# Local attention on one core: weighted values by features, weights divided before their transposition, one wide exponential, and another order of TensorE's stages

## The chip, the cores and the metric

The kernel runs on one core of a Trainium2 chip. The metric is the time of one execution on the device, in microseconds; less is better. TensorE multiplies and transposes, ScalarE (ACT) and VectorE (DVE) empty its results out of PSUM and do the elementwise work, GpSimd (POOL) takes elementwise work between tiles in SBUF, and SyncE (SP) issues the DMAs.

## What is computed

All data are float32. The input is 8 sequences of 512 tokens with 128 features. First comes a linear attention with a Taylor feature map (16 heads), then six layers of local attention and feed-forward. The change lies in the local attention:

```python
H, HD, W = 16, 64, 32                      # heads, features of a head, window
for i in range(6):
    x = attn_layer(shift_tokens(x), Wqkv[i], q_scale[i], k_scale[i], Wo[i]) + x
    x = ffn_layer(shift_tokens(x), ...) + x

# attn_layer: project, unit length and scale of q and k, rotary, then in windows of 32 tokens
sim  = einsum('bhwie,bhwje->bhwij', bq, bk2) * 8     # 32 queries by 64 keys (own and last window)
sim  = where(mask, -max, sim)
attn = softmax(sim, -1)
out  = einsum('bhwij,bhwje->bhwie', attn, bv2)
return out.reshape(b, n, 1024) @ Wo
```

## The kernel before

After the linear attention the kernel works in blocks of 128 tokens. There are 4 blocks in a sequence, 8 sequences and 6 layers: 192 blocks. The running activations stay in SBUF, features by tokens, one `state` tile for each sequence.

The steps of a block are functions, and one loop over t calls them, each with a lag: `at(t, lag, step)` runs a step for block t - lag. So one pass of the loop holds steps of several blocks, and it is what the document calls a block's time. TensorE's instructions are issued in exactly the order in which this loop writes them (`manual_schedule` for PE). The other engines' orders are made by a scheduler; `tc.high_priority()` and `issue_behind(later, earlier)` push it. Every engine runs its own list strictly in order.

The steps, with their lags before the change:

- `proj` (lag 0, twice: for q and for k): two matmuls into a PSUM tile of tag "mm" (line 451). VectorE makes the two rotary products from it (lines 459 and 467), ScalarE two squares (line 475), POOL adds the products (line 482).
- `sum_squares`, `unit_length` (lag 0): VectorE sums the squares (line 485); ScalarE takes Ln and Exp (lines 96 and 98); POOL clips (line 495) and multiplies q and k by it (line 498).
- `values`, `spread` (lag 0): two matmuls into "mm" (line 509), one copy by ScalarE (line 514), then 10 DMAs (8 and two memsets in a sequence's first block) that lay the windows out in `v2` with heads of even pairs on partitions 0 to 63 and of odd ones on 64 to 127.
- `by_features` (lag 1): 16 transposes of q and k, in four PSUM tiles of tag "tr" with four transposes each (line 70), each emptied by a ScalarE copy (line 548). POOL copies the last 32 tokens' keys for the next block (line 551).
- `masked`, `scores` (lag 1): ScalarE writes the mask into a PSUM tile of tag "s" (line 558), 64 small matmuls add the scores `sp` to it (line 572); VectorE takes the negated maxima (line 580); ScalarE takes 16 exponentials with the maxima as bias (line 584, 64 columns each); VectorE sums and inverts (lines 590 and 591).
- `by_keys`, `weigh_values` (lag 2): 8 transposes of the weights `pe`, in two "tr" tiles, copied by ScalarE (line 602); 64 small matmuls weigh the values into `po`, tokens by features, tag "s" (line 613); VectorE divides by the sums (line 621) into `on`.
- `out_by_features` (lag 2): 8 transposes of `on` in two "tr" tiles, copied by ScalarE (line 635).
- `out_project` (lag 3): 8 matmuls into `py`, tag "s" (line 642); VectorE adds it to the state (line 647).
- Feed-forward, in a sequence's last block alone, so each in one pass of four: `feed_norm` (4 transposes `nx` of the state into "mm", statistics by VectorE, lines 107 and 109, Ln and Exp by ScalarE, lines 96 and 98, normalising by VectorE, line 112), `feed_first` (4 transposes), `feed_middle` (six matmuls, lines 667 and 669, with Gelu at 673, for which ScalarE loads another table, and loads the old one back, lines 76 and 82), `feed_last` (three matmuls, line 702).

PSUM has three tags: "mm" with two buffers of 4 KB a partition, "tr" with two of 2 KB, "s" with one of 4 KB. A stage that takes a buffer waits until the tile before the last one of its tag has been read. A float32 matmul shows as two matmul records, each with its load of weights.

`addr_align` puts filler instructions into TensorE's list (lines 668, 671, 780 and 782).

Of the kernel before, what the change touches and what calls it, by code (L numbers as in the profile page):

```python
# [15 lines left out]
P = 128  # L16
# [7 lines left out]
FILL = 16  # L24
IN_STEP = 98
# [3 lines left out]
def sandwich_kernel(ctx: ExitStack, tc: tile.TileContext, ins: dict, out: bass.AP):  # L29
# [43 lines left out]
    tables, exps, divisions, copies, pcopies, maxima = [], [], [], [], [], []  # L73
# [365 lines left out]
    def proj(u, s):  # L439

        L, b, j = u["L"], u["b"], u["j"]
        wqkv, tab = L["wqkv"], L["tab"]
        lhs = state[b][:, j * P : (j + 1) * P]
        if s == 0:
            u["ss"] = f2.tile([P, 2, H], F32, tag="ss", name="ss")
            u["qk"] = f2.tile([P, 2, H, 2, HF], F32, tag="qk", name="qk")
        ss, qk = u["ss"], u["qk"]

        ps = psum.tile([P, 2, H, HF], F32, tag="mm", name="mm")
        for a in range(2):  # L450
            nc.tensor.matmul(  # L451
                ps[:, a].rearrange("p h d -> p (h d)"), lhs, wqkv[:, s, a, :], start=True, stop=True
            )
        sq = f2.tile([P, H, 2, HF], F32, tag="sq", name="sq")
        t1 = f2.tile([P, 2, H, HF], F32, tag="t1", name="t1")
        t2 = f2.tile([P, 2, H, HF], F32, tag="t2", name="t2")

        def turned():
            nc.vector.tensor_tensor(  # L459
                t2, ps[:, ::-1],  # L460
                tab[:, 2 * s + 1, j, :].rearrange("p (a d) -> p a d", a=2).unsqueeze(2)
                .to_broadcast([P, 2, H, HF]),
                ALU.mult,
            )

        def straight():
            nc.vector.tensor_tensor(  # L467
                t1, ps,
                tab[:, 2 * s, j, :].rearrange("p (a d) -> p a d", a=2).unsqueeze(2)
                .to_broadcast([P, 2, H, HF]),  # L470
                ALU.mult,
            )

        def squared(a):
            nc.scalar.activation(sq[:, :, a, :], ps[:, a], AF.Square)  # L475

        turned()
        straight()
        squared(0)
        squared(1)  # L480
        u["sq", s] = sq
        nc.gpsimd.tensor_tensor(qk[:, s].rearrange("p h a d -> p a h d"), t1, t2, ALU.add)  # L482

    def sum_squares(u, s):
        su = nc.vector.tensor_reduce(  # L485
            u["ss"][:, s], u["sq", s].rearrange("p h a d -> p h (a d)"), AX.X, ALU.add
        )
        if divisions:
            issue_behind(su, divisions[-1])
# [22 lines left out]
    def spread(u):  # L512
        j, v0 = u["j"], u["v0"]
        cp = nc.scalar.copy(v0, u.pop("v0ps"))
        if copies:
            issue_behind(cp, copies[-1])
# [36 lines left out]
    def masked(u):  # L553
# [7 lines left out]
        issue_behind(sd, copies[-1])  # L561

    def scores(u):
# [18 lines left out]
        for pair in range(NP):  # L582
            for p in range(2):
                ex = nc.scalar.activation(  # L584
                    pe[:, pair, p, :], sp[:, p, pair, :], AF.Exp, bias=mx[:, p, pair : pair + 1]
                )
                issue_behind(ex, tables[-1])
        exps.append(ex)
        su = f2.tile([P, NP, 2], F32, tag="su", name="su")
        nc.vector.tensor_reduce(su, pe, AX.X, ALU.add)  # L590
        nc.vector.reciprocal(su, su)
        u["pe"], u["su"] = pe, su
# [11 lines left out]
    def weigh_values(u):  # L604


        v2, pT, su = u["v2"], u["pT"], u["su"]
        po = psum.tile([P, 2, NP, HD], F32, tag="s", name="po", bufs=1)
        for pair in range(NP):
            for w in range(4):  # L610
                for p in range(2):
                    r = slice(HD * p, HD * (p + 1))
                    nc.tensor.matmul(  # L613
                        po[W * w : W * (w + 1), p, pair, :],
                        pT[r, pair, W * w : W * (w + 1)],
                        v2[r, w, HD * pair : HD * (pair + 1)],
                        start=(pair == 0), stop=True, skip_group_check=True,
                    )
        u["on"] = on = f1.tile([P, NP, 2, HD], F32, tag="on", name="on")
        with tc.high_priority():  # L620
            dv = nc.vector.tensor_tensor(
                on.rearrange("t c p d -> t p c d"), po,
                su.rearrange("t c p -> t p c").unsqueeze(3).to_broadcast([P, 2, NP, HD]), ALU.mult,
            )
        divisions.append(dv)

    def out_by_features(u):
        on = u["on"]
        u["oT"] = oT = f1.tile([P, NP, P], F32, tag="oT", name="oT")
        for c in range(0, NP, 4):  # L630
            ps = psum.tile([P, 4, P], F32, tag="tr", name="tr")
            for i in range(4):
                transposed(ps[:, i, :], on[:, c + i].rearrange("p a d -> p (a d)"), P, P)
            with tc.high_priority():
                nc.scalar.copy(oT[:, c : c + 4, :], ps)  # L635

    def out_project(u):

        L, b, j, oT = u["L"], u["b"], u["j"], u["oT"]
        py = psum.tile([P, P], F32, tag="s", name="py", bufs=1)  # L640
        for c in range(NP):
            nc.tensor.matmul(py, L["wo"][:, c, :], oT[:, c, :], start=(c == 0), stop=(c == NP - 1))  # L642
# [7 lines left out]
    def feed_norm(u):  # L650
# [6 lines left out]
        u["normed"] = layer_norm(f2, xn, ps, NB, by_log=True, later=True)  # L657
# [4 lines left out]
    def feed_hidden(u, c):  # L662
# [5 lines left out]
        nc.tensor.addr_align(FILL, offset=FILL // 2)  # L668
        nc.tensor.matmul(pg[:cn, 1], w1[:, c0 : c0 + cn], xnT, start=True, stop=True)  # L669
        if c < NCH - 1:  # L670
            nc.tensor.addr_align(FILL, offset=FILL // 2)
# [85 lines left out]
    with tc.manual_schedule(engines={mybir.EngineType.PE}):  # L757
# [8 lines left out]
        for t in range(len(units) + 7):  # L766
# [6 lines left out]

            gelus = 0 <= t - 5 < len(units) and units[t - 5]["j"] == NB - 1
            at(t, 0, proj, 0)
            at(t, 0, proj, 1)


            if t % NB == 1 and NB < t < len(units):
                nc.tensor.addr_align(128, offset=IN_STEP)  # L780
            if t % NB == 3 and NB < t < len(units):
                nc.tensor.addr_align(FILL)
            at(t, 2, by_keys)
            if gelus:
                gelu_only()
            at(t, 3, out_project)
# [6 lines left out]
            at(t, 2, weigh_values)  # L793
            at(t, 1, by_features, 4, 0)
            at(t, 1, masked)
            at(t, 0, values)
# [6 lines left out]
            at(t, 1, by_features, 4, 1)  # L803
            at(t, 0, spread)
            at(t, 3, feed_norm, ends=True)
            at(t, 4, feed_first, ends=True)

            ends = 9 + NB * B * (DEPTH - 1) <= t < len(units) + 5
            after = 10 + NB * B * (DEPTH - 1) <= t < len(units) + 6
            if after:  # L810
                at(t, 10, out_roots, ends=True)
            if ends:
                at(t, 9, out_by_tokens, ends=True)
                at(t, 9, out_stats, ends=True)
            at(t, 5, feed_middle, ends=True)
            if gelus:
                at(t, 0, unit_length)
            at(t, 6, feed_last, ends=True)
            at(t, 1, scores)
            if after:  # L820
                at(t, 10, store, ends=True)
            if t == len(units) + 5:
                at(t, 6, out_by_tokens)
                at(t, 6, out_stats)
                at(t, 6, out_roots)
                at(t, 6, store, False)
            at(t, 3, feed_normed, ends=True)
            at(t, 2, out_by_features)


# [98 lines left out]
```

## Time and profile before

| what | value |
|---|---|
| runs | 3638.80, 3639.42, 3642.14 us; median 3639.42 |
| span of the profiled execution | 3641.2 us |
| mean granted TensorE clock | 0.993 of full speed |
| first projection of the local attention | 479.0 us after the start |
| busy in 600 to 3500 us, of 2900: PE, DVE, ACT, POOL | 2892, 2351, 2356, 1708 us |
| sixteen transposes of q and k, `tr<-ident,qk` | 3072 of 276 ns mean |
| division, line 621 | 192 of 1225 ns |
| exponentials, line 584 | 3072 of 381 ns, 652.0 us busy |

The profiled execution's own time is not given beside its span; its span lies inside the three runs, 0.9 us under the longest. A group's row gives busy time (overlaps counted once), the mean length of one instruction, then the idle time ahead of it and what ended that. Matmuls are pipelined, so the mean length of one is far above the distance from one to the next. A timeline's row gives start, length, engine, line, tile and how many instructions are merged in it.

### The profile page before, as it was taken

To read this page: it belongs to the slowest core of one execution; us is meant where nothing else is said; L and a number is where in the kernel's file an instruction comes from. 1 tells how busy PE (TensorE), PEld (TensorE's weight loads), DVE (VectorE), ACT (ScalarE), POOL (GpSimd) and SP (SyncE) were. 2 spreads that over 40 slices of the span, in tenths; PEclk is the share of its full clock that TensorE was granted. 3 is DMA by queue.
4 is the path that set the end of the run, shared out by engine and by line. 5 is a ranking of instruction groups with operands and counts; after the bars stand their busy time and mean duration, and the time that the engine had idled before them with its cause. 6 is when DMAs were issued, how large, how long until landed. Compare 5 with 4: busy or idle time off the path is not lost.

```text
span 3641.2 us, 153034 instructions
## 1 busy us (share of the span) xinstructions
PE 3575.2 (98%) x65184; PEld 2404.3 (66%) x65184; DVE 2796.4 (77%) x3915; ACT 2765.6 (76%) x6864; POOL 1843.6 (51%) x1311
## 2 busy tenths in 40 slices
PE   8999989999999999999999999999999999999997
PEld 4555556666766666676766766667676676766765
DVE  4555567887878788787887878878787887878885
ACT  4555557787888888888787888888878787887875
POOL 0000045555655556555565655556555565556652
PEclk9999999999999999999999999999999999999998
DMA  3121132222232222232222322223222222222221
GB/s 109 46 53 47 42 89 68 65 65 69 79 77 72 65 64 71 77 81 68 61 69 68 87 72 69 65 65 86 71 71 69 60 70 64 66 68 73 74 74 47
DMA packets 158598, 250.73 MB, mean 69 GB/s; under 512 B 33774, under 2 KB 54508, under 8 KB 157164
## 3 DMA queue, kind: packets, MB, share of 16 engines
q1 hardware_dynamic: 157932, 240.93, 25.2%
q8 instruction: 530, 8.68, 1.0%
q14 instruction: 136, 1.11, 0.1%
HBM read 41.31 MB, written 4.46 MB: 13 GB/s over the span
## 4 chain that ended last, share of the span: by engine, by line
PE 87%; ACT 9%; DVE 2%; issue 1%; DMA 1%; POOL 0%; SPq 0%; POOLq 0%; DVEq 0%; ACTq 0%
PE tr L70 19%; PE mm L451 14%; PE py L642 10%; PE mm L509 9%; PE po L613 8%; PE sp L572 6%; ACT pe L584 4%; PE mm L667 4%; PE mm L669 4%; PE y L299 3%; PE py L702 3%; PE sc L269 2%; PE po L348 2%; ACT L76 1%; PE vv L247 1%; ACT oT L635 1%
## 5 line engine op out<-in xcount | busy, mean ns | idle before, releaser
L482 POOL TENSOR_TENSOR qk<-t,t 128x1024 f32<-128x1024 f32 x384 | 910.9, 2372 | 619.1 <-DVE t L467 424.7
L498 POOL TENSOR_TENSOR qk<-qk,ss 128x1024 f32<-128x1024 f32 x384 | 722.4, 1902 | 16.0
L451 PE MATMUL mm<-wqkv,state 128*128 128x512 f32 x1536 | 700.3, 596 | 0.6 <-issue 0.6
L584 ACT ACTIVATE pe<-sp,mx 128x64 f32<-128x64 f32 x3072 | 652.0, 381 | 2.4 <-DVE mx L580 2.3
L459 DVE TENSOR_TENSOR t<-mm,tab 128x1024 f32<-128x1024 f32 x384 | 468.3, 1219 | 220.3 <-PE mm L451 214.9
L475 ACT ACTIVATE sq<-mm 128x512 f32<-128x512 f32 x768 | 420.6, 605 | 127.4 <-DVE t L467 120.9
L467 DVE TENSOR_TENSOR t<-mm,tab 128x1024 f32<-128x1024 f32 x384 | 468.1, 1219 | 5.9
L451 PEld LDWEIGHTS mm<-wqkv,state 128*128 128x128 f32 x1536 | 273.1, 190 | 289.8 <-issue 242.4
L485 DVE TENSOR_REDUCE ss<-sq 128x16 f32<-128x1024 f32 x384 | 448.4, 1209 | 0.1
L70 PE MATMUL tr<-ident,qk 128*128 128x128 f32 x3072 | 440.9, 276 | 1.8 <-ACT qT L548 0.8
L70 PEld LDWEIGHTS tr<-ident,qk 128*128 128x128 f32 x3072 | 351.3, 141 | 120.7 <-issue 56.3
L642 PE MATMUL py<-oT,wo 128*128 128x128 f32 x3072 | 379.3, 277 | 0.3 <-ACT oT L635 0.3
L642 PEld LDWEIGHTS py<-oT,wo 128*128 128x128 f32 x3072 | 368.1, 196 | 0.5 <-ACT oT L635 0.5
L509 PE MATMUL mm<-wqkv,state 128*128 128x512 f32 x768 | 362.9, 595 | 2.6 <-DVE t L467 2.6
L635 ACT COPY oT<-tr 128x512 f32<-128x512 f32 x384 | 205.5, 587 | 168.1 <-PE tr L70 165.5
L572 PEld LDWEIGHTS sp<-kT,qT 64*32 64x32 f32 x24576 | 264.2, 105 | 91.3 <-issue 54.3
L613 PE MATMUL po<-v,pT 64*32 64x64 f32 x24576 | 297.0, 225 | 9.6 <-issue 3.9
L548 ACT COPY qT<-tr 128x512 f32<-128x512 f32 x384 | 226.3, 589 | 99.6 <-PE tr L70 99.1
L613 PEld LDWEIGHTS po<-v,pT 64*32 64x32 f32 x24576 | 268.8, 105 | 46.0 <-PE tr L70 24.6
L572 PE MATMUL sp<-kT,qT 64*32 64x64 f32 x24576 | 297.6, 225 | 0.3 <-issue 0.3
L495 POOL TENSOR_SCALAR ss<-ss 128x32 f32<-128x32 f32 x192 | 54.7, 285 | 478.7 <-ACT ss L98 470.8
L548 ACT COPY kT<-tr 128x512 f32<-128x512 f32 x384 | 225.6, 588 | 74.8 <-PE tr L70 74.5
(110 smaller groups left out, 5243.9 us busy)
## 6 DMA issues: line engine op xcount, KB each, us to landing
v<-v SPq DMA_DIRECT2D x1152, 128.0 KB
v<-v SPq DMA_DIRECT2D x672, 64.0 KB
rs<-roots SPq DMA_DIRECT2D x64, 256.0 KB
wqkv<-in_L_ffn_Wqkv_dram SPq DMA_DIRECT2D x6, 1536.0 KB
wo<-in_L_ffn_Wo_dram SPq DMA_DIRECT2D x6, 512.0 KB
xin<-_attn_hidden_states_dram SPq DMA_DIRECT2D x8, 256.0 KB
xr<-_attn_hidden_states_dram SPq DMA_DIRECT2D x8, 256.0 KB
x<-xr SPq DMA_DIRECT2D x8, 256.0 KB
```

Source lines behind the costliest of these rows:

```text
L70: nc.tensor.transpose(ps[:cols, :rows], src, ident[:rows, :rows])
L451: nc.tensor.matmul(ps[:, a].rearrange("p h d -> p (h d)"), lhs, wqkv[:, s, a, :], start=True, stop=True)
L459: nc.vector.tensor_tensor(t2, ps[:, ::-1], tab[:, 2 * s + 1, j, :].rearrange("p (a d) -> p a d", a=2).unsqueeze(2) .to_broadcast([P, 2, H, ...
L467: nc.vector.tensor_tensor(t1, ps, tab[:, 2 * s, j, :].rearrange("p (a d) -> p a d", a=2).unsqueeze(2) .to_broadcast([P, 2, H, HF]), ALU.mult,)
L482: nc.gpsimd.tensor_tensor(qk[:, s].rearrange("p h a d -> p a h d"), t1, t2, ALU.add)
L498: nc.gpsimd.tensor_tensor(t, t, ss[:, i, :].unsqueeze(2).to_broadcast([P, H, HD]), ALU.mult)
L509: nc.tensor.matmul(ps[:, p, :], lhs, L["wqkv"][:, 2, p, :], start=True, stop=True)
L548: copies.append(nc.scalar.copy(dst, ps))
L572: nc.tensor.matmul(sp[W * w : W * (w + 1), p, pair, :], qT[HD * p : HD * (p + 1), pair, W * w : W * (w + 1)], kT[HD * p : HD * (p + 1), pa ...
L584: ex = nc.scalar.activation(pe[:, pair, p, :], sp[:, p, pair, :], AF.Exp, bias=mx[:, p, pair : pair + 1])
L613: nc.tensor.matmul(po[W * w : W * (w + 1), p, pair, :], pT[r, pair, W * w : W * (w + 1)], v2[r, w, HD * pair : HD * (pair + 1)], start=(pa ...
L642: nc.tensor.matmul(py, L["wo"][:, c, :], oT[:, c, :], start=(c == 0), stop=(c == NP - 1))
```

## The change

- The weights are divided by their sums (in a new step `divided`, lag 2, on POOL) before `by_keys` transposes them. The maxima are subtracted by VectorE, and one exponential of 128x1024 runs in place.
- `weigh_values` takes the values as stationary operand and the weights as moving one, so that `po` comes out as features by tokens, in a tile of tag "mm". One ScalarE copy of 128x1024 makes `oT` from it; `out_by_features` with its transposes is gone. The rows of `Wo` are put in another order on the host to fit.
- `py` moves from tag "s" to "tr". `nx` is copied to SBUF by ScalarE and normalised from there.
- The filler instructions are gone, as is an ordering of the sums of squares behind the division and one of the value copy behind the copies of q and k; the mask is ordered behind the squares.
- The order of the stages in a pass and their lags are new: the sixteen transposes of q and k stand together, `by_keys` lies between the two projections (lag 3), `values` comes at the end with lag 2, and what follows has one lag more.

```diff
     def scores(u):
...
-        for pair in range(NP):
-            for p in range(2):
-                ex = nc.scalar.activation(
-                    pe[:, pair, p, :], sp[:, p, pair, :], AF.Exp, bias=mx[:, p, pair : pair + 1]
-                )
-                issue_behind(ex, tables[-1])
+        with tc.high_priority():
+            nc.vector.tensor_tensor(
+                pe.rearrange("t c p k -> t p c k"), sp,
+                mx.unsqueeze(3).to_broadcast([P, 2, NP, 2 * W]), ALU.add,
+            )
+        pf = pe.rearrange("t c p k -> t (c p k)")
+        ex = nc.scalar.activation(pf, pf, AF.Exp)
+        issue_behind(ex, tables[-1])
         exps.append(ex)
+        u["pe"] = pe
+
+    def divided(u):
+        pe = u["pe"]
         su = f2.tile([P, NP, 2], F32, tag="su", name="su")
         nc.vector.tensor_reduce(su, pe, AX.X, ALU.add)
         nc.vector.reciprocal(su, su)
-        u["pe"], u["su"] = pe, su
+        nc.gpsimd.tensor_tensor(pe, pe, su.unsqueeze(3).to_broadcast([P, NP, 2, 2 * W]), ALU.mult)
...
-        po = psum.tile([P, 2, NP, HD], F32, tag="s", name="po", bufs=1)
-        for pair in range(NP):
+        po = psum.tile([P, 2, NQ, P], F32, tag="mm", name="po")
+        for i in range(NQ):
             for w in range(4):
-                for p in range(2):
-                    r = slice(HD * p, HD * (p + 1))
-                    nc.tensor.matmul(
-                        po[W * w : W * (w + 1), p, pair, :],
-                        pT[r, pair, W * w : W * (w + 1)],
-                        v2[r, w, HD * pair : HD * (pair + 1)],
-                        start=(pair == 0), stop=True, skip_group_check=True,
-                    )
-        u["on"] = on = f1.tile([P, NP, 2, HD], F32, tag="on", name="on")
...
+                for pair in (2 * i, 2 * i + 1):
+                    for p in range(2):
+                        r = slice(HD * p, HD * (p + 1))
+                        c = (p + pair) % 2
+                        nc.tensor.matmul(
+                            po[HD * c : HD * (c + 1), p, i, W * w : W * (w + 1)],
+                            v2[r, w, HD * pair : HD * (pair + 1)],
+                            pT[r, pair, W * w : W * (w + 1)],
+                            start=(i == 0 and w == 0), stop=True, skip_group_check=True,
+                        )
+        u["oT"] = oT = f1.tile([P, 2, NQ, P], F32, tag=("on", "oT")[u["j"] % 2], name="oT")
+        nc.scalar.copy(oT, po)
...
-        py = psum.tile([P, P], F32, tag="s", name="py", bufs=1)
+        py = psum.tile([P, P], F32, tag="tr", name="py")
...
-        for t in range(len(units) + 7):
+        for t in range(len(units) + 8):
...
             at(t, 0, proj, 0)
+            at(t, 3, by_keys)
             at(t, 0, proj, 1)
-            at(t, 2, by_keys)
+            at(t, 2, divided)
...
-            at(t, 3, out_project)
...
             at(t, 1, by_features, 0)
-            at(t, 2, weigh_values)
             at(t, 1, by_features, 4, 0)
+            at(t, 1, by_features, 4, 1)
+            at(t, 4, out_project)
+            at(t, 3, weigh_values)
             at(t, 1, masked)
-            at(t, 0, values)
...
-            at(t, 1, by_features, 4, 1)
-            at(t, 0, spread)
...
+            at(t, 2, values)
+            at(t, 2, spread)
             at(t, 1, scores)
...
-            at(t, 2, out_by_features)
```

## The prediction

> **What bounds the kernel now.** I read the page first (shares, slices, chain), then the sums by window, then the timeline of TensorE over one block, then ScalarE beside it. A block is one pass of the loop over t; 192 of them hold attention's second half, and the 180 whole ones between 600 and 3500 us last 16.11 us each, from first projection to first projection.
>
> ```profile
> PE 3575.2 (98%) x65184; PEld 2404.3 (66%) x65184; DVE 2796.4 (77%) x3915; ACT 2765.6 (76%) x6864; POOL 1843.6 (51%) x1311
> ...
> PE 87%; ACT 9%; DVE 2%; issue 1%; DMA 1%; POOL 0%; SPq 0%; POOLq 0%; DVEq 0%; ACTq 0%
> ```
>
> TensorE is busy nearly always and is 87% of the chain. In the middle it has no idle time at all: 2892 of 2900 us, at full clock.
>
> ```profile
> 600.00:3500.00 2900.00, 2892.33 (x58069) 1998.83 (x58068) 2351.29 (x3020) 2356.14 (x6093) 1707.75 (x1199) 1.00 0.27 70
> ```
>
> So a block is a sum of TensorE stages, and a stage's price is the distance from its start to the next stage's start (the printed length has the pipeline's tail in it). The timeline of one block:
>
> ```profile
> 1499.06 3.79 PE L451 MATMUL mm<-wqkv,state 128*128 128x512 f32 x8
> 1502.68 1.04 PE L70 MATMUL tr<-ident,pe 128*128 128x128 f32 x8
> 1503.56 1.95 PE L642 MATMUL py<-oT,wo 128*128 128x128 f32 x16
> 1505.35 1.04 PE L70 MATMUL tr<-ident,qk 128*128 128x128 f32 x8
> 1506.31 1.53 PE L613 MATMUL po<-v,pT 64*32 64x64 f32 x128
> 1507.77 0.66 PE L70 MATMUL tr<-ident,qk 128*128 128x128 f32 x4
> 1508.27 1.88 PE L509 MATMUL mm<-wqkv,state 128*128 128x512 f32 x4
> 1509.99 0.60 PE L70 MATMUL tr<-ident,qk 128*128 128x128 f32 x4
> 1510.42 0.60 PE L70 MATMUL tr<-ident,xn 128*128 128x128 f32 x4
> 1510.95 1.49 PE L572 MATMUL sp<-kT,qT 64*32 64x64 f32 x128
> 1512.37 1.09 PE L70 MATMUL tr<-ident,on 128*128 128x128 f32 x8
> ```
>
> Two things to see. The "on" transposes, which the change removes, take 13.30 - 12.37 = 0.93 us. And the transposes come two tiles (8 of them) at a time at most, with a stage of 1.4 us or more behind: the tag "tr" has two PSUM buffers, and ScalarE must empty one before a third tile can start. What emptying takes:
>
> ```profile
> 1505.98 0.58 ACT L548 COPY qT<-tr 128x512 f32<-128x512 f32 x1 [0.59 <-PE tr L70]
> 1506.47 0.58 ACT L548 COPY kT<-tr 128x512 f32<-128x512 f32 x1
> 1507.73 1.08 ACT L475 ACTIVATE sq<-mm 128x512 f32<-128x512 f32 x2 [0.67 <-DVE t L467]
> ```
>
> A tile is 0.44 us on TensorE (1510.42 - 1509.99). Its copy starts 0.2 us after it (tile ended about 1505.79, copy 1505.98), copies follow each other by 0.49 us, one lasts 0.58 us, and TensorE goes on about 0.05 us after its end (the value copy ends at 1526.44, the waiting matmul starts at 1526.49). Two tiles thus need 0.44 + 0.2 + 0.58 + 0.05 = 1.27 us per buffer where TensorE alone needs 0.88.
>
> **The change, per block.**
>
> (a) The "on" transposes go: **-0.93**.
>
> (b) The weighted values (po) swap operands: weights 64x64 instead of 64x32, moving 64x32 instead of 64x64, and four regions of the array side by side instead of eight.
>
> ```profile
> L613 PEld LDWEIGHTS po<-v,pT 64*32 64x32 f32 x24576 | 268.8, 105 | 46.0 <-PE tr L70 24.6 <-issue 20.4 <-PE py L642 0.9
> ...
> L299 PEld LDWEIGHTS y<-am,tv 128*64 128x64 f32 x1024 | 64.3, 137 | 86.3 <-issue 66.6 <-PE vv L247 8.0 <-DVE am L282 0.9
> ...
> L269 PEld LDWEIGHTS sc<-tq,tk 32*128 32x128 f32 x1024 | 49.5, 190 | 60.1 <-ACT am L278 36.8 <-issue 14.3 <-ACT rt L331 4.2
> ```
>
> Loads of 32, 64 and 128 columns take 105, 137 and 190 ns: some 0.87 ns a column over a fixed latency, so 64 columns are about 54 ns of streaming. Where loads bound (line 226, 4 moving columns), 128-column loads start 112 ns apart, 107 plus 5, and multiplying hides behind the next load. So a region takes 54 + 4 = 58 ns per pass, and 128 passes over four regions 32 x 58 = 1.86 us; with the start 1.90, against 1.48 now (mean of 180 blocks): **+0.42**. Bounds: 1.48, today's pace of 11 ns a matmul, which already needs loads faster than those rows, so that a gain is excluded; 32 x 85 = 2.72 if load and multiply (27 ns) don't overlap within a region. I take 1.90 because lines 226 and 70 show the overlap.
>
> On (b) a rule speaks louder against the change than my rows. The Trainium skill, "TensorE: Matmul & The Clock Gate", section "Back-to-back issue gap", has about 25 ns from start to start however few columns move; by it the 128 would take 3.2 us, and the block 1.3 us more than I take. This trace disagrees: in po matmuls of different regions start 7 to 17 ns apart, 11 on average.
>
> (c) Waits of today that go. Summed over its stages' shortest distances a block would be 15.61 us, so 0.50 is waiting and filler. The largest single cause in the view of waits is
>
> ```profile
> PEld tr L70 <- ACT pe L584: 114.8, 418, 1.8
> ```
>
> transposes of the weights that wait for the sixteen exponentials (3.39 us a block). They become one, near 1.02 us as the 128x1024 copies of lines 514 and 558, and have a whole block more. The filler instructions go too (0.19 us in one projection of four, 3.63 against 3.44). I take **-0.45**, between 0 and -0.50; all sixteen transposes of q and k are priced anew in (d).
>
> (d) The sixteen transposes now stand together, and out_project's py moves into the same two buffers, as fifth tile. Block clock by the rows above, 0 at the first projection: projection to 1.72, pe transposes to 2.59, projection to 4.31, tile q0 to 4.75, q1 to 5.19. ScalarE copies q0 from 4.95 and q1 from 5.44. Tile q2 waits for q0's copy: 4.95 + 0.58 + 0.05 = 5.58, instead of 5.19; q3 for q1's: 6.07, ready 6.51. In the built order a square of line 475 stands between q1's and q2's copy on ScalarE: 5.93, so q2's copy starts at 6.42, ends at 7.00, and py starts at 7.05 instead of 4.31 + 4 x 0.44 = 6.07. A wait of 0.98. That square waits for VectorE's second rotary product: maximum from 0.3, subtraction, two products at 1.14 us pitch, ended 4.94; it just fits. In one block of four, four normalising instructions (1.36 us, line 112) stand in front of it: q2's copy is at 6.74, the wait 1.30. In another the table load (1.28 us) stands ahead of q0's copy: 5.55 instead of 4.95, the wait 1.58. Mean **+1.21**. Below 0.78 it can't go, with ScalarE free for nothing else.
>
> (e) po now shares the "mm" ring of two with the projections, nx and the values, its reader is one oT copy (1.02). In the block of four that has nx, the values take po's buffer. On ScalarE the logarithm of line 96 is ahead of the oT copy, and waits for the last sum of squares: VectorE's row from 0.3 is max, subtraction, four products, sum, sum of squares, state (0.58), reciprocal (0.28), sum of squares, ended near 11.5. Logarithm 0.27, copy to 12.80, values at 12.85; TensorE is there at 7.05 + 1.79 + 1.90 + 0.53 = 11.27. 1.58 in one block of four: **+0.40**, bounds 0 and 0.5.
>
> (f) Hidden: the division as a multiplication on POOL, 1.88 us as line 498's; POOL goes from 9.5 to 11.4 of over 16 us. Behind it wait the two unit-length products, done near 17.5, needed at the next block's 21. If that cover went, their lateness would land on q0. VectorE's subtraction replaces its division, 1.22 each. The xn copy (0.58) runs beside the values. Values two blocks later leave their DMAs the time from 14.5 to the next block's po near 25.5; SP's queue holds the same ten per block.
>
> Sum: -0.93 + 0.42 - 0.45 + 1.21 + 0.40 = +0.65 us a block, times 192 = 125 us. The loop has one pass more to drain: +2 (between 0 and one block, 16). **3641 + 127 = 3768 us.** The sum stands on the profiled span, 3641.2; the three runs were 3638.8, 3639.4 and 3642.1, so the median lies 2 us under it, less than the rounding of my terms.
>
> **Rivals.**
>
> *Faster.* TensorE does not wait for the ring: copies keep up. Then (a) to (c) give -0.96 a block, with 0.25 left of (d) and nothing of (e) -0.71, 136 us: 3505. It decides once (d) and (e) together cost under 0.96. For it: ScalarE is freed of 2.4 us a block. Against it: 1.27 against 0.88, which no freed time changes. 13%.
>
> *Level.* (d) at its least, 0.78, (e) at 0.15: 3641 within 0.2%. 4%.
>
> *Slower still.* Load and multiply in series, po 2.72: +157, 3925. For it: in po a region comes round every 8 x 11 = 88 ns, near 27 + 5 + 53. 6%.
>
> *Slower, but less: the new po costs nothing*, since instruction issue bounds it and not columns: -0.42, 3687. For it: the same 256 instructions. 13%. That the change doesn't do what it says is excluded by the built order: the "on" transposes are gone and the sixteen stand together.
>
> **How the numbers follow.** Forecast 64%, 3768. The range 3640 to 3880 holds it with its errors (a quarter of (d), all of (c)), the free po and the level case; 19% is left out. Faster by over 0.2% (some 7 us, about what measuring can tell) 14%, within 3%, slower 83%.
>
> **What will show it.** TensorE idle or stretched at the third tile of q and k and at py, released by ScalarE's qT and kT copies, 1.0 to 1.6 us a block; values behind nx waiting for oT in one block of four, 1.6 us; po's starts spread over 1.7 to 2.0 us; blocks of 16.7 to 16.8 us. I am wrong if py follows the transposes without a gap, if po takes over 2.5 us, or if the pe transposes wait for POOL.

## The result, and the profile after

| | before | after |
|---|---|---|
| median of the runs | 3640.78 us (3638.8 to 3647.42) | 3848.18 us (3843.12 to 3851.75) |
| span of the profiled execution | 3641.2 us | 3841.4 us |
| mean granted TensorE clock | 0.993 | 0.993 |
| one block, first projection to first projection | 16.11 us | 17.18 us |

The change makes the kernel slower: the ratio is 1.0567, with an interval of 1.0552 to 1.0582. The direction and the range were right. The rise is 207 us where 127 were forecast.

The busy time of the engines and the chain's shares, from the page of the kernel after:

```profile
PE 3589.7 (93%) x63648; PEld 2355.0 (61%) x63648; DVE 2752.0 (72%) x3915; ACT 2312.7 (60%) x3840; POOL 2190.3 (57%) x1503
...
PE 66%; ACT 14%; DVE 13%; issue 2%; POOL 2%; DMA 2%; SPq 1%; DVEq 0%; POOLq 0%; ACTq 0%
```

ScalarE lost 453 us of work and stands in the chain with 14% instead of 9%. TensorE now has idle time in the middle (2917 of 3100 us busy between 600 and 3700), and where it waits in the blocks it is mostly for ScalarE. (VectorE's share of the chain rises more, from 2% to 13%, but no wait of TensorE's on VectorE reaches 8 us in the view of waits.) The view of waits for TensorE names the places; its columns are the total in us, how often, and the longest:

```profile
PE tr L68 <- ACT qT L542: 82.5, 193, 1.0
PE py L630 <- ACT qT L542: 65.4, 189, 1.4
PE mm L505 <- ACT oT L623: 38.3, 47, 0.9
```

The first two are the third tile of q and k and py, both waiting for copies out of the two "tr" buffers. The third is the values behind nx. All three were forecast. The timeline of TensorE over one block, and at the end a stretch with nx:

```profile
1499.80 1.04 PE L68 MATMUL tr<-ident,qk 128*128 128x128 f32 x8
1501.07 1.15 PE L68 MATMUL tr<-ident,qk 128*128 128x128 f32 x8 [0.24 <-ACT qT L542]
1502.54 2.05 PE L630 MATMUL py<-oT,wo 128*128 128x128 f32 x16 [0.32 <-ACT qT L542]
1504.52 2.07 PE L616 MATMUL po<-pT,v 64*64 64x32 f32 x128
1506.52 0.66 PE L68 MATMUL tr<-ident,xn 128*128 128x128 f32 x4
1507.02 1.88 PE L505 MATMUL mm<-wqkv,state 128*128 128x512 f32 x4
1508.83 1.48 PE L567 MATMUL sp<-kT,qT 64*32 64x64 f32 x128
1510.24 1.98 PE L449 MATMUL mm<-wqkv,state 128*128 128x512 f32 x4
...
1559.97 0.66 PE L68 MATMUL nx<-ident,state 128*128 128x128 f32 x4
1561.46 1.98 PE L505 MATMUL mm<-wqkv,state 128*128 128x512 f32 x4 [0.83 <-ACT oT L623]
```

From first to last start, q, k and the way to py take 1502.54 - 1499.80 = 2.74 us, where four tiles without a wait are 1.74. Note how little of that loss of 1.00 stands in brackets: 0.24 + 0.32 us. The rest is in the distances: the length of a row has the pipeline's tail in it (1.04 us for a pair of tiles whose successor could start after 0.87), so a stage is late before its bracket counts, and the pair that restarts after a wait is longer itself (1.15). Po takes 2.00 us and py 1.98. ScalarE over the same time:

```profile
1500.43 0.59 ACT L542 COPY qT<-tr 128x512 f32<-128x512 f32 x1 [0.56 <-PE tr L68]
1500.92 0.59 ACT L542 COPY kT<-tr 128x512 f32<-128x512 f32 x1
1501.40 0.61 ACT L473 ACTIVATE sq<-mm 128x512 f32<-128x512 f32 x1
1501.89 0.60 ACT L542 COPY qT<-tr 128x512 f32<-128x512 f32 x1
```

The first copy starts 0.63 us after the first tile (0.44 of transposes, then 0.2), copies follow each other by 0.49, and the square sits where the built order had it, between the second tile's copy and the third's. Py starts 0.05 us after that third copy's end (1502.49).

The mean distance from each stage to the next, in us per block, for 180 blocks before and 180 after:

| stage | before | after | difference |
|---|---|---|---|
| two projections | 3.484 | 3.539 | +0.06 |
| pe transposes | 0.961 | 0.873 | -0.09 |
| 16 transposes of q and k | 1.960 | 2.958 | +1.00 |
| py | 1.787 | 1.982 | +0.19 |
| po | 1.476 | 2.058 | +0.58 |
| values | 1.719 | 1.846 | +0.13 |
| sp | 1.479 | 1.419 | -0.06 |
| on transposes | 0.929 | 0 | -0.93 |
| nx (one block of four) | 0.133 | 0.369 | +0.24 |
| xn and the rest of feed-forward | 2.18 | 2.14 | -0.04 |

Before rounding the differences come to +1.07, as do the blocks' own lengths. From the ninth block to the last, 183 blocks of 1.07 are 196 us, of 200 us between the two spans; the rest lies at the two ends, where stages are missing.

### The profile page after: what moved, and what is told of

The parts are those of the page before. It is cut to its first block, busy times and chain, and to the rows that moved or that the text cites. A ratio compares the mean times of both kernels' runs of the same rounds, so it can differ in the third digit from the quotient of the medians.

```text
span 3841.4 us, 142603 instructions
## 1 busy us (share of the span) xinstructions
PE 3589.7 (93%) x63648; PEld 2355.0 (61%) x63648; DVE 2752.0 (72%) x3915; ACT 2312.7 (60%) x3840; POOL 2190.3 (57%) x1503
## 4 chain that ended last, share of the span: by engine, by line
PE 66%; ACT 14%; DVE 13%; issue 2%; POOL 2%; DMA 2%; SPq 1%; DVEq 0%; POOLq 0%; ACTq 0%
PE mm L449 11%; PE mm L505 9%; PE po L616 8%; PE py L630 8%; PE sp L567 7%; PE tr L68 5%; ACT qT L542 4%; PE mm L658 4%; PE py L690 3%; PE mm L659 3%; PE y L297 3%; DVE t L457 3%; DVE t L465 2%; DVE ss L483 2%; PE sc L267 2%
## 5 line engine op out<-in xcount | busy, mean ns | idle before, releaser
L449 PE MATMUL mm<-wqkv,state 128*128 128x512 f32 x1536 | 743.0, 606 | 2.6 <-DVE t L465 2.6
L603 ACT COPY pT<-tr 128x512 f32<-128x512 f32 x384 | 206.6, 590 | 492.8 <-PE tr L68 492.8
L68 PE MATMUL tr<-ident,qk 128*128 128x128 f32 x3072 | 419.4, 279 | 83.6 <-ACT qT L542 82.5
L575 DVE TENSOR_REDUCE mx<-sp 128x16 f32<-128x1024 f32 x192 | 235.1, 1225 | 341.2 <-PE sp L567 341.2
L630 PE MATMUL py<-oT,wo 128*128 128x128 f32 x3072 | 393.8, 281 | 66.7 <-ACT qT L542 65.4
L473 ACT ACTIVATE sq<-mm 128x512 f32<-128x512 f32 x768 | 434.9, 637 | 19.2 <-DVE t L465 18.7
L616 PE MATMUL po<-pT,v 64*64 64x32 f32 x24576 | 406.8, 220 | 12.3 <-DMA v<-v 7.5
L593 POOL TENSOR_TENSOR pe<-pe,su 128x1024 f32<-128x1024 f32 x192 | 365.4, 1903 | 72.1 <-DVE su L592 72.1
L616 PEld LDWEIGHTS po<-pT,v 64*64 64x64 f32 x24576 | 382.3, 135 | 38.7 <-DMA v<-v 9.4
L505 PE MATMUL mm<-wqkv,state 128*128 128x512 f32 x768 | 368.0, 601 | 39.6 <-ACT oT L623 38.3
L510 ACT COPY v<-mm 128x1024 f32<-128x1024 f32 x192 | 193.7, 1009 | 179.1 <-PE mm L505 177.5
```

Of the source, the lines that this page charges most:

```text
L68: nc.tensor.transpose(ps[:cols, :rows], src, ident[:rows, :rows])
L449: nc.tensor.matmul(ps[:, a].rearrange("p h d -> p (h d)"), lhs, wqkv[:, s, a, :], start=True, stop=True)
L473: squares_.append(nc.scalar.activation(sq[:, :, a, :], ps[:, a], AF.Square))
L505: nc.tensor.matmul(ps[:, p, :], lhs, L["wqkv"][:, 2, p, :], start=True, stop=True)
L616: nc.tensor.matmul(po[HD * c : HD * (c + 1), p, i, W * w : W * (w + 1)], v2[r, w, HD * pair : HD * (pair + 1)], pT[r, pair, W * w : W * (w ...
L630: nc.tensor.matmul(py, L["wo"][:, c, :], oT[:, c // NQ, c % NQ, :], start=(c == 0), stop=(c == NP - 1))
```

## The experiments

Each was timed beside runs of the kernel before on the same chip, and ratios are to that. "After" and "before" name the kernel that was edited. The first two leave out part of the mask: py stands with a start flag in the bank into which the mask is written next (in experiment 1 py at 1501.34 us, the mask at 1504.01) and to which the scores are then added. That the flag is the cause is inferred from experiment 3, which does without it and computes what the reference asks. The times of the first two stand for the order and the buffers alone.

**1. After, py in a buffer of its own (tag "s" as before).**

```diff
-        py = psum.tile([P, P], F32, tag="tr", name="py")
+        py = psum.tile([P, P], F32, tag="s", name="py", bufs=1)
```

> The changed kernel with py back in tag s, at its place behind the sixteen transposes; the scheduler now also puts the oT copy ahead of the logarithm in the nx block. Ring theory: py no longer waits for the third tile's copy (0.57 us a block) and its first load is hidden again (0.10), the third tile still waits for the first copy (0.39), and the nx block's wait goes (0.24 a block): -0.91 us a block, 3848 - 174 = 3674. Rival (the longer time is in the new po and in stages that start behind it, waits only move): nothing gained beyond 40 us, 3810 or more.

Measured: 3737.54 us, ratio 1.0262 [1.0247, 1.0277]. Half of the rise goes, 111 us of 207. The transposes with their waits fall from 2.96 to 2.44 us a block; the third tile's wait stays at 81.5 us in all, py's is gone. Py itself now takes 1.88 us from its start to po's. That the time is 63 us above the ring theory's lies mostly at nx: only 0.06 of its 0.24 us went, and the values still wait 26.7 us in all for the oT copy.

**2. The same, and py between the two pairs of tiles.** `by_features` of q's and k's first tiles, `out_project`, then the other two.

```diff
             at(t, 1, by_features, 0)
+            at(t, 4, out_project)
             at(t, 1, by_features, 4, 0)
             at(t, 1, by_features, 4, 1)
-            at(t, 4, out_project)
```

> As the run before, and py stands between the second and the third tile of q and k. Ring theory: the wait of the third tile goes as well, 1.21 + 0.10 + 0.24 = 1.55 us a block, 3848 - 297 = 3551, under the kernel before; transposes of q and k cost 4 x 0.44 = 1.75 us a block in all. Rival (another engine's chain, POOL with its 11.4 us or VectorE, bounds the block as soon as the ring doesn't): 3640 or more, with waits for POOL's or VectorE's work at the transposes.

Measured: 3608.92 us, ratio 0.9914 [0.9897, 0.993]; the rise is gone, and 32 us more. This is TensorE's timeline:

```profile
1507.02 1.95 PE L630 MATMUL py<-oT,wo 128*128 128x128 f32 x16
1508.81 1.04 PE L68 MATMUL tr<-ident,qk 128*128 128x128 f32 x8
1509.78 2.07 PE L616 MATMUL po<-pT,v 64*64 64x32 f32 x128
```

Of the waits for copies of q and k under 3 us are left in all: py's 1.79 us cover ScalarE's two copies. Since only py's buffer and place differ from the kernel after, the ring with the stages crowded on it, and the slower start of what waited, cost 239 us, more than the whole rise. The time came out 58 us above what I expected, and that lies in two places: at nx, where 0.19 of the 0.24 us stay (the values wait 28.3 us in all for the oT copy), and at the transposes, 1.86 us instead of 1.75, as two tiles ahead of po take 0.97 us and ahead of py 0.87 (an edge, see below).

**3. The same order with the mask whole.** VectorE clears py, and the matmuls accumulate without a start flag.

```diff
+        with tc.high_priority():
+            nc.vector.memset(py, 0.0)
...
-                py, L["wo"][:, c, :], oT[:, c // NQ, c % NQ, :], start=(c == 0), stop=(c == NP - 1)
+                py, L["wo"][:, c, :], oT[:, c // NQ, c % NQ, :], start=False, stop=True,
+                skip_group_check=True,
```

> As the run with py between the second and the third tile, in tag s, but py is added to a tile that VectorE has set to zero instead of starting anew, so that the bank's mark of what has been written stays and the scores are added to the mask as in the changed kernel. Theory: the 128x128 memset (some 0.2 us on VectorE, which idles a quarter of the time) is hidden: 3609 to 3625, under the kernel before. Rival: the memset and the state's addition on VectorE delay the rotary products and with them the squares ahead of the copies of q and k: 3650 or more.

Measured: 3619.93 us, ratio 0.9946 [0.9932, 0.9959], as expected: 11 us above the last one, with the memset. So the missing mask did not make the gain.

**4. Before, with nothing changed but the order: the 16 transposes together behind py.**

```diff
             at(t, 1, by_features, 0)
+            at(t, 1, by_features, 4, 0)
+            at(t, 1, by_features, 4, 1)
             at(t, 2, weigh_values)
-            at(t, 1, by_features, 4, 0)
...
-            at(t, 1, by_features, 4, 1)
```

> The kernel before with one part of the change alone: the sixteen transposes of q and k together, behind py (which keeps its own buffer), then po, values and the rest. Ring theory: the third tile waits 0.39 to 0.45 us a block for the first copy, nothing else waits for the ring: 3641 + 80 = 3720. Rival (the order costs nothing in the old kernel, since its other waits shrink by as much): 3640 within 15.

Measured: 3801.15 us, ratio 1.0443 [1.0428, 1.0459]. The order of the transposes alone, in a kernel with sixteen exponentials, old po and on transposes, costs 160 us, twice what was expected. TensorE's timeline, in a block with feed-forward:

```profile
1511.21 1.48 PE L613 MATMUL po<-v,pT 64*32 64x64 f32 x128
1512.62 1.98 PE L509 MATMUL mm<-wqkv,state 128*128 128x512 f32 x4
1514.44 1.02 PE L667 MATMUL mm<-xnT,w 128*128 128x512 f32 x2
```

The transposes rise from 1.96 to 2.52 us a block, by the third tile's wait for qT (77.2 us in all, 191 times); that is 107 of the 160 us. Most of the rest is at the projections (+0.12 us a block, with 18.0 us of waits for xn), the values (+0.10) and the pe transposes (+0.08). In the lines a second thing is to be seen: the values, the same four matmuls as ever, take 1514.44 - 1512.62 = 1.82 us. In the kernel before they take 1.72 in every block, behind transposes; here they stand behind po.

**5. After, with the logarithm of the unit length ordered behind the oT copy on ScalarE.**

```diff
+        if behind is not None:
+            issue_behind(ln, behind)
...
+        inverse_root(ss, ss, behind=ocopies[-1] if ocopies else None)
...
+        ocopies.append(nc.scalar.copy(oT, po))
```

> The changed kernel with one ordering more: the logarithm of unit length stands behind the oT copy on ScalarE. Theory: in the nx block the values wait for po's buffer 0.83 us of idle and some 0.1 of restart because that copy is behind the logarithm; -0.24 us a block, 3848 - 45 = 3803, and the ring waits stay. Rival (the copy itself is too late, po has only just ended): no more than 10 us gained.

Measured: 3831.24 us, ratio 1.0523 [1.0507, 1.0539]: 17 us, between the two. The distance from nx to the values falls from 1.48 to 1.20 us, and the longest wait from 0.9 to 0.5. So the logarithm's place explains 0.28 us of some 0.95; the rest is the copy itself, which starts 0.14 us after nx does (1560.15 against 1560.01) and takes 1.01, while nx covers only 0.49.

**6. Kernel 3, with nx in the ring "tr" instead of "mm".**

```diff
-        ps = psum.tile([P, NB, P], F32, tag="mm", name="nx")
+        ps = psum.tile([P, NB, P], F32, tag="tr", name="nx")
```

> The correct version with py between the transposes (3620), and nx takes a buffer of tag tr instead of mm, so that the values no longer come back to po's buffer in the nx block. Ring theory: the 0.86 us that nx is longer than its 0.53 in one block of four go: 3620 - 41 = 3579. Rival (nx then waits for the copy of the third tile in the same way): 3610 or more.

Measured: 3607.98 us, ratio 0.9908 [0.9891, 0.9924]. The values' wait for oT is gone, as the theory said: nx to values is 0.49 instead of 1.43 us. But only 12 us of the expected 41 arrive. The four tiles of q and k rise from 1.87 to 1.93 us a block and xn from 0.54 to 0.81: part of the wait moved to the other ring. This version computes what the reference asks, and is the fastest of this study, 35 us under the kernel before.

**7. Kernel 3, with values ahead of po.** Po and sp, of 256 instructions each (128 matmuls and as many loads), become neighbours.

```diff
-            at(t, 3, weigh_values)
...
             at(t, 2, values)
             at(t, 2, spread)
+            at(t, 3, weigh_values)
```

> The run above, and values stand ahead of po, so that po and the scores, both stages of small matmuls, follow each other. Edge theory: a stage of full-size matmuls beside a stage of small ones costs 0.09 to 0.10 us at each edge, because its first load (or the small stage's first) can't be hidden; here one to two edges of four go: 17 to 35 us less than the run above. Rival: values now need the second projection's buffer 2 us earlier, and the squares and VectorE have not read it yet: 30 us or more above the run above, with values waiting for a square.

Measured: 4064.17 us, ratio 1.1154 [1.1136, 1.1171]. 444 us slower than kernel 3. The edge theory fell; the rival's wait is there (values wait 43.8 us in all for squares), but it is a tenth of the loss. The timeline of TensorE:

```profile
604.98 1.23 PE L567 MATMUL sp<-kT,qT 64*32 64x64 f32 x96
607.51 0.46 PE L567 MATMUL sp<-kT,qT 64*32 64x64 f32 x32 [1.31 <-issue]
```

In the middle of sp, with no operand missing, TensorE stands still; sp takes 3.14 us a block instead of 1.42. The releaser "issue" means that nothing on another engine ended the wait. The trace's DMA records have something there: a packet of the queue "instruction" runs from 605.13 to 606.25. This led to the next experiments.

**8. Before, without the fillers** (all calls of `addr_align` taken out).

```diff
-        nc.tensor.addr_align(FILL, offset=FILL // 2)
...
-            if t % NB == 1 and NB < t < len(units):
-                nc.tensor.addr_align(128, offset=IN_STEP)
-            if t % NB == 3 and NB < t < len(units):
-                nc.tensor.addr_align(FILL)
```

> The kernel before without its filler instructions, nothing else. Forecast's reading: they cost 0.05 us a block in the projections and up to 0.08 in the feed-forward: 3641 - 10 to - 25. Rival: they cost nothing net, as the distance they add stands where TensorE waits in any case or where instructions arrive late: 3641 within 7, or more.

Measured: 3749.41 us, ratio 1.03 [1.0282, 1.0318]. Instructions that do nothing are worth 108 us. TensorE's timeline:

```profile
692.79 1.23 PE L613 MATMUL po<-v,pT 64*32 64x64 f32 x100
696.23 0.32 PE L613 MATMUL po<-v,pT 64*32 64x64 f32 x9 [2.21 <-issue]
```

Again a packet of the instruction queue falls into the gap, from 693.57 to 694.78. TensorE goes on 1.4 us after such a packet's end, by the median of the stalls of this run and of the last; for four fifths of some 200 stalls it is 1.26 to 1.54 us, which chance would not give, as the packets come some 7 us apart. Behind the stall TensorE is also slower for a while. The same four matmuls of the values, which otherwise take 1.72 us up to the next stage's start, take 3.00 (699.98 - 696.98), and the view of a window gives the granted clock there as half (0.50, third number from the end):

```profile
696.98 3.21 PE L509 MATMUL mm<-wqkv,state 128*128 128x512 f32 x4
697.38:700.79 3.41, 3.41 (x8) 1.70 (x7) 2.71 (x3) 1.40 (x2) 0.00 (x0) 0.50 0.18 43
```

Between 600 and 3500 us this run has 15 such stretches, 51 us in all; the kernels before and after have none there. If all that TensorE does in them takes twice as long, some 26 of the 108 us are of this kind (an estimate from these rows, an upper one).

**9. Before, with the fillers at another offset** (64 instructions fewer in the whole program, of 153034).

```diff
-IN_STEP = 98
+IN_STEP = 34
```

> The kernel before with the constant that places its filler once in four blocks, 98, changed to 34; as many filler places as before. Fetch theory (TensorE's instructions come in pieces of 256, one piece ahead; where a piece begins inside a stage of 256 small-matmul instructions decides whether the next one arrives in time): stalls inside po or the scores come back, 20 us or more, with a fetch just before each. Rival (the filler helps by the time that it takes, or by its number): 3641 within 7.

Measured: 3833.96 us, ratio 1.0524 [1.0502, 1.0546]. One constant costs 191 us. The work and its order are the same; what differs is the position in TensorE's list at which each stage begins. Waits on "issue" come to 143 us at po, values, transposes and sp. The largest in TensorE's view of waits:

```profile
PE po L613 <- issue: 87.8, 46, 2.5
```

**10. Before, with VectorE's subtraction and the wide exponential alone.**

```diff
-                ex = nc.scalar.activation(
-                    pe[:, pair, p, :], sp[:, p, pair, :], AF.Exp, bias=mx[:, p, pair : pair + 1]
...
+            nc.vector.tensor_tensor(
+                pe.rearrange("t c p k -> t p c k"), sp,
+                mx.unsqueeze(3).to_broadcast([P, 2, NP, 2 * W]), ALU.add,
+            )
+        pf = pe.rearrange("t c p k -> t (c p k)")
+        ex = nc.scalar.activation(pf, pf, AF.Exp)
...
```

> The kernel before with one part alone: VectorE subtracts the maxima and one wide exponential follows. Theory: the pe transposes' wait for exponentials goes (0.09 us a block, 17 us), and 1.14 us more on VectorE a block, busy 81% there, costs about as much: 3641 within 40, with the wait at the pe transposes gone. Rival (VectorE becomes the bound): 3700 or more, with TensorE waiting for rotary products or the division.

Measured: 3875.02 us, ratio 1.0646 [1.0616, 1.0676]. Neither theory's number. The wait of the pe transposes is gone as (c) had it (0.96 to 0.88 us a block), but TensorE's view of waits shows two new things:

```profile
PE po L615 <- issue: 125.5, 63, 4.0
PE mm L451 <- DVE xn L112: 49.6, 47, 1.1
```

The first is the stall of experiments 7 to 9, though no line of TensorE's stages was edited; but TensorE's own list has 16 instructions fewer in the trace (70470, loads and sequencer, against 70486), so that stages begin at other places of it. The second is the rival's: VectorE's extra pass over the scores makes its normalising late for the projection. TensorE also spends 96 us at half clock here. How much of the 232 us each has was not separated further.

**11. After, with sixteen exponentials again.** The reverse of 10's edit.

> The changed kernel with one part undone: sixteen exponentials instead of subtraction and one wide one. Theory: on ScalarE fourteen of them now stand ahead of the first copy of q, which comes near 5.3 instead of 4.95, and the third tile's copy near 6.7 instead of 6.4: 0.2 to 0.4 us a block, 3890 to 3925. Rival (ScalarE has time enough): 3848 within 15. The 400 us that the same edit cost with py in tag s are not expected here, as py then waited for the scores' bank.

Measured: 3880.98 us, ratio 1.065 [1.0633, 1.0667], 33 us slower than the kernel after: between the theories. The distance from nx to values is 1.98 us instead of 1.48: in the block that I looked at, both of unit length's activations stand ahead of the oT copy, the first 0.54 us after nx's start instead of 0.31, and the copy 0.93 after it instead of 0.44. The theory's longer transposes of q and k did not come (2.93 us a block, 2.96 in the kernel after). In the kernel after, the wide exponential is a gain.

**12. Kernel 3, with sixteen exponentials.**

> The first run of this call, with the sixteen exponentials of the kernel before instead of subtraction and one wide exponential. Theory: with the ring spread ScalarE is not the bound, and the wide exponential alone is worth nothing: within 15 us of the first run of this call. Rival: 2.4 us more on ScalarE ahead of the copies of q and k come back as waits of TensorE for qT and kT: 40 us or more above it.

Measured: 4039.28 us, ratio 1.1095 [1.1078, 1.1111]: 419 us above, in the rival's range, but the wait is another. TensorE's view of waits:

```profile
PE py L630 <- DVE py L628: 356.3, 190, 4.4
```

Py shares its bank with the scores. The sixteen exponentials read the scores from PSUM until 1505.86 us in the stretch I looked at, VectorE's memset of py follows at 1506.08, the matmul at 1506.30. The memset stands in VectorE's list behind the second rotary product, which ends at 1506.05; an earlier place could give 0.2 us at most, as the exponentials hold the bank until 1505.86. With the wide exponential, VectorE's subtraction empties the bank early: in experiment 3 the memset starts 1.16 us (median) after it. So the wide exponential is what makes py's place in experiment 3 possible.

## Why the prediction was right or wrong

The steps of the sum, per block:

| step | forecast | measured |
|---|---|---|
| (a) on transposes | -0.93 | -0.93 |
| (b) po | +0.42 | +0.58 |
| (c) old waits and fillers | -0.45 | -0.46 |
| (d) ring of two, five tiles | +1.21 | +1.21 |
| (e) values behind nx | +0.40 | +0.24 |
| edges between stages, and a restart | no term | +0.43 |
| sum | +0.65 | +1.07 |

The direction and the range held. Among the priced terms (b) is 0.16 too small and (e) 0.16 too large, which cancel by luck; what the sum misses, 0.42, is the row that has no term.

(a) and (d) came out as worked out: 2.958 - 4 x 0.436 is 1.21. Experiments 1, 2 and 4 show the mechanism of (d), by taking it away and by making it alone. Inside, the split was a little different: three blocks of four take 2.74 us (a wait of 1.00, forecast 0.98), and the one with the table load 3.49 (1.75, forecast 1.58); the 1.30 for the block with normalising did not show. So the wait and its cause are as forecast, and that the mean agrees in its last digit is luck.

(b) The step failed in size. The pace was right: the starts of four regions repeat every 58.5 ns, 58 were worked out, and 32 rounds are 1.87 us. (The 54 ns for 64 columns are half of the 107; with the 0.87 ns a column that stands beside them it would have been 56, and a round 60.) But the whole stage takes 2.00 at its best and 2.06 on average; the start that I priced at 0.04 is 0.13, and waits add 0.06, among them 7.5 us in the whole run for the DMAs of v that (f) had as hidden. The Trainium skill's rule of about 25 ns from start to start ("TensorE: Matmul & The Clock Gate", "Back-to-back issue gap") would have given 3.2 us, an estimate from that page; measured are 15.6 ns a matmul, and the rows were the better guide. The rival in which the new po costs nothing is refuted.

(c) held in its sum, with the parts that can be told apart: pe transposes 0.09, sp 0.06, feed-forward 0.04, fillers 0.05 and 0.22 in the old q and k transposes (1.960 - 4 x 0.436). Its make-up was another than forecast: the wait for the exponentials, named as the largest, was worth 0.09, and 0.15 of the 0.22 are edges beside po (below).

(e) The mechanism was there, the size was off: I had the logarithm make the values 1.58 us late, and the distance from nx to them is 0.94 us longer than before. ScalarE in the block with nx that the timeline above shows (line 94 is the logarithm now):

```profile
1560.28 0.23 ACT L94 ACTIVATE ss<-ss 128x32 f32<-128x32 f32 x1 [1.47 <-DVE ss L483]
1560.41 0.99 ACT L623 COPY oT<-po 128x1024 f32<-128x1024 f32 x1
```

The logarithm waits for VectorE's sum and holds the copy, as worked out. But the copy starts 0.44 us after nx (1559.97), where I had 1.04 (11.78 against 10.74 on the block's clock, which starts with the projection at 1548.81). TensorE is 0.42 later there (11.16): py takes 0.19 more than I gave it, po 0.12, and the projection behind sp 0.10. The copy comes 0.18 earlier (11.60): it starts 0.13 behind the logarithm's start, not 0.27. By experiment 5 the logarithm has 0.28 of the 0.94.

**The step that failed most is the sum itself**: I priced each stage at the distance that it had in the old order, with nothing for its new neighbours, and a stage's distance depends on its neighbours. What this left out is 0.43 us a block, some 82 us; the forecast is 80 us too low. Py shows it in three steps: 1.79 us between transposes (before, experiments 2 and 3), 1.88 when po follows (experiment 1), 1.98 when it also starts after a wait (after). Values are 1.72 between transposes, 1.82 behind po in the old kernel (experiment 4), and 1.81 ahead of sp in the kernel after (1.91 where they also start after a wait, behind nx). The projection behind sp is 1.82 where behind transposes it is 1.72. Each time a stage of small matmuls borders on one of full size, 0.09 to 0.10 us go. (Experiment 7 was to test this, and its stalls cover it; so the edges rest on the distances in these traces.) The old order had groups of transposes there, and they do not spare the edge: in the trace before, two tiles ahead of po take 0.97 us instead of 0.87 and xn ahead of sp 0.53 instead of 0.44; behind po a tile takes 0.49, and on behind sp 0.93 instead of 0.87. The forecast let such edges go with (a) and (c) and put nothing for the new ones, which account for py +0.19, values +0.13 and projections +0.11 (0.06 in the table, and the fillers' 0.05 that went there).

The rival in which the copies keep up is refuted by the waits; the level one, by (d)'s 1.21 and (e)'s 0.24, where it needs 0.78 and 0.15; the slower one, by po's 2.06 us.

What I never considered are the fillers as more than 0.05 us. By experiments 8 and 9 I take it that they keep TensorE's list in step with its fetching, and the change takes them out. In the kernel after this costs little: TensorE's waits on "issue" are 3.4 us at po and 3.4 at sp in the whole run, and it has no stretch at half clock between 600 and 3500 us. That po, of 2.0 us, with values between it and sp, leaves the fetch time enough, is argued from experiment 7, where kernel 3's list with po and sp adjacent stalls; it was not tried with fillers in the kernel after.

## What to carry to other kernels

When a stage order is rewritten, price three things beside the instructions: how many tiles in a row go through a ring and what stands between the third and the first copy; the edges, by the distance that the stage has beside such neighbours elsewhere in the trace; and where the instruction list is cut. A ring of two needs work of another kind between its pairs: here 1.8 us of py moved ahead by two tiles was worth 118 to 129 us (experiments 1 to 3). A change that is slower as it stands can hold a faster one: with py between the pairs and nx in the other ring it is 35 us faster than the kernel before.

## What the runs showed of the hardware that I had not expected

- **Instruction fetching can stop TensorE.** The page's row for the queue "instruction" has 530 packets and 8.68 MB before (16.4 KB each). The Trainium skill, "Runtime: NRT & Kernel Launch", section "Instruction fetch mechanics", has blocks of this size, of 256 instructions, and calls the crossing mostly hidden. The runs agree on the size, and disagree on the rest where stages of 256 short instructions follow each other: po and sp use up as much in 1.4 to 2.0 us, a packet takes about 1.1 us, and from its start to TensorE's going on it is 2.4 us by the median (half of the stalls 2.35 to 2.64). The price was 108 us without fillers, 191 us with fillers at another offset, and 270 of 444 us with po and sp adjacent (waits of sp on "issue"). That the cuts between blocks of instructions lie where the stalls are is inferred from these three and from the packets' times; the cuts themselves are in no trace.
- **After a stop the granted clock can be half for 3.4 us.** Between 600 and 3500 us the kernels before and after have no such stretch, experiment 8 has 51 us of them, 9 has 44, 7 has 82, 10 has 96 and 12 has 99. So a stop can cost more than its own length; not every stop was followed by one (15 stretches in experiment 8).
- **A change on one engine can move another's stalls.** Experiment 10 edited VectorE and ScalarE alone, TensorE's list became 16 instructions shorter, and po's issue stalls rose to 125.5 us. Such an experiment does not price its edit alone.
- **Edges between full and small matmuls cost 0.09 to 0.10 us (0.06 where transposes follow small ones), and a restart after a wait 0.10 us.** After a wait the second matmul of py starts 213 ns behind the first, without one 112.
